# Attention: where the halves of side products and the parts of the shift stand among the slots

## The chip, the cores and the metric

The kernel runs on one core of a Trainium2 chip. A core has TensorE for matmuls (PE in the profile; its weight loads are PEld), VectorE (DVE), ScalarE (ACT), GpSimd (POOL) and SyncE (SP, which issues DMAs). Each works through its own instructions in their order and waits on semaphores for the others. The metric is device time in microseconds; lower is better.

## The reference

The whole program is a network of four layers on x of shape (4, 128, 64, 64): seven phases, one after the other. The change lies in the phase `attention`, the first half of the last layer: attention over the 4096 pixels of each of 4 images, with 4 heads of 32 channels, on a layer-normed x, and added to x.

```python
qkv = jnp.einsum('oc,bchw->bohw', w_qkv, x)
q, k, v = jnp.split(qkv, 3, axis=1)
...
q = to_heads(q) * SCALE
...
sim = jnp.einsum('bhdi,bhdj->bhij', q, k)
attn = jax.nn.softmax(sim, axis=-1)
out = jnp.einsum('bhij,bhdj->bhid', attn, v)
...
out = jnp.einsum('oc,bchw->bohw', w_out, out) + b_out[None, :, None, None]
```

and `x = x + _L3_conv_ref(_ln_c(x), ...)`. All of it is float32.

## The kernel before

**Tiles.** A batch (image) `b` has 4096 queries, in NCH = 8 chunks of CH = 512, and 4096 keys, in NT = 32 tiles of P = 128. A *block* `g` is one chunk of queries of one batch: 32 blocks in all, `b, c = divmod(g, NCH)`. A *slot* `t` is one tile of keys within a block: 32 slots in a block, 1024 in all.

**A slot.** The main loop (L2094 to L2132) records, in each slot and in this order: `scores(g, t)`, 4 matmuls (one a head, on four row groups of PE) into two *pairs*, PSUM tiles of two banks that hold two heads each (L1983 to L1988), and one exponential of ACT for each pair, into `att_ex` (L1990), with a bias `att_shift`; then `product` of the slot before (L2002), 4 matmuls of its exponentials with the values into `att_pv`; then `add_up` of the slot before, which adds its exponentials up: on DVE (L2021), or, for every fourth slot, by a DMA that accumulates, issued by POOL (L2019). `att_ex` has six buffers.

**PSUM.** There are 8 banks: three pairs (six banks), one bank `att_m`, one for `att_pv`. A call of `pair()` takes the next of the three. Each slot takes two.

**Side work.** What else must be computed on PE goes through the one bank `att_m` and is cut into *halves* of some 4 to 8 matmuls, each with its slot; after the second half, DVE or ACT reads the bank:

- `side`, the generator `project` (L1823): for the next batch, centred squares (ACT squares them) and their variances, an inverse root (one square root on ACT, four reciprocals on DVE, DMAs that spread it), then keys and queries of 8 chunks. It goes one step further in each slot of `USES` (L2088, L2116) in blocks 1 to 6 of a batch. Its steps in the second half also issue DMAs on SP.
- `values` (L1922): the values of 8 chunks, in slots of `USES` in block 0 and block 7.
- `total` (L2030): sums of the added-up exponentials over the keys, for the block before, after `join` has added DVE's part and the DMAs' part (L2024, a DMA issued by POOL); then `totalled` (a copy and two reductions), four `invert` (reciprocals, L2052), `scale_hidden` (a multiply on POOL, L2055), and `project_out` (L2064) with its addition to x. These stand in `queue` by slots after the block's last (L2136 to L2143).
- the shift of the next block: `begin` (L1946), twice, each with two small matmuls of scores into a pair and a maximum over them on DVE (L1962); then `gather_shift` (L1968) in slot 25 and `spread_shift` (L1976) in slot 27.

In block 0 a different rule, by `t % 4`, gives slots two halves each and every fourth slot none (L2110 to L2115).

**Order.** Inside `tc.manual_schedule` the instructions of PE, ACT, DVE and POOL stand in the order in which the program records them; the framework adds the semaphores.

Before the change, the slots with halves are 2 and 3, 6 and 7, 14 and 15, 18 and 19, 30 and 31 (`USES`), 10 and 11 (`total`), 22 and 23 (`project_out`); `begin` is in 19 and 23.

## Time and profile before

| | |
|---|---|
| median of 3 runs | 6059.14 us (6057.93 to 6070.12) |
| profiled execution, its own time | 6065.83 us |
| its span | 6063.9 us |
| mean granted clock of TensorE | 0.972 |
| stretch of the slots of attention | 3203 to 5656 us |
| in it, busy | PE 2445, DVE 2007, ACT 2163, POOL 304 us of 2453 |

The profile is of one execution. Times in a timeline are in us from the start of the span: start, length, engine, line, operation, tiles that it writes and reads, count; rows that follow each other on one engine are merged, and in brackets stands the idle time of the engine ahead of it with what ended it. In a group's row, "x8192 | 1291.7, 643 | 7.0 <-..." is the count, the busy time in us, the mean length in ns, and the idle time just before, with what ended it. Matmuls are pipelined, so that their lengths overlap; what a group takes is read from the start of the next one.

### The profile page before, as it was taken

What the parts mean: (1) busy time and instruction counts of PE and PEld (TensorE: products, weight loads), DVE (VectorE), ACT (ScalarE), POOL (GpSimd) and SP (SyncE); (2) the same over time, 40 slices, a digit from 0 to 9 for tenths busy, and PEclk for the clock granted to TensorE, in tenths of its full rate; (3) what the DMA queues carried; (4) which work ended last, traced back from release to release, by engine and by line L of the source; (5) the groups of instructions that cost most, each with busy time, mean ns of one, the idle gap of its engine ahead of it and who ended that gap; (6) DMA issues with size and microseconds to landing.
All of it is one profiled execution on the core that took longest, in us unless ns stands there. A gap on an engine that the chain in (4) does not pass through costs nothing. (4 is left out here: it accounts for less than half of the span.)

```text
span 6063.9 us, 97913 instructions
## 1 busy us (share of the span) xinstructions
PE 5701.8 (94%) x39923; PEld 2251.2 (37%) x39923; DVE 4383.8 (72%) x4739; ACT 3378.6 (56%) x4224; POOL 2056.5 (34%) x2015
## 2 busy tenths in 40 slices
PE   8999999879999988879979999999999999999799
PEld 2222222447667666433343222322232223222233
DVE  6888887456767666356446788888888888888666
ACT  4444444333323222421337888888888888999421
POOL 3989897027777777200000111111111111111000
PEclk9999999989999999989989999999999999999899
DMA  6434432068787877550274566656665666666200
GB/s 214 98 80 84 96 68 53 1 169 245 233 250 225 248 228 211 164 182 0 88 263 116 128 152 149 138 127 151 149 140 126 148 147 144 130 130 133 60 25 26
DMA packets 291038, 836.36 MB, mean 138 GB/s; under 512 B 43356, under 2 KB 117596, under 8 KB 244492
## 3 DMA queue, kind: packets, MB, share of 16 engines
q0 software_dynamic: 109568, 505.75, 35.0%
q1 hardware_dynamic: 181004, 324.17, 18.8%
q8 instruction: 320, 5.24, 0.4%
q14 instruction: 146, 1.20, 0.1%
HBM read 416.71 MB, written 111.10 MB: 87 GB/s over the span
## 5 line engine op out<-in xcount | busy, mean ns | idle before, releaser
L1990 ACT ACTIVATE att_ex<-att_sc,att_shift 128x1024 f32<-128x1024 f32 x2048 | 2141.6, 1111 | 288.9 <-PE att_sc L1986 173.5
L2021 DVE TENSOR_TENSOR att_dve<-att_dve,att_ex 128x2048 f32<-128x2048 f32 x704 | 1631.2, 2317 | 159.1 <-ACT att_ex L1990 134.1
L1986 PE MATMUL att_sc<-att_q,att_k 32*128 32x512 f32 x8192 | 1291.7, 643 | 7.0 <-ACT att_ex L1990 7.0
L2002 PE MATMUL att_pv<-att_ex,att_vals 128*32 128x512 f32 x8192 | 1095.9, 606 | 0.0
L969 POOL DMA_INDIRECT dcn_g<-dcn_table,dcn_idx x896 | 850.1, 949 | 363.9 <-issue 154.1
L412 DVE SCALAR_TENSOR_TENSOR inv_prod<-inv_pk,bspan,inv_seen 128x512 f32<-128x512 f32 (+1 forms) x1120 | 774.5, 743 | 140.2 <-PE inv_pk L399 139.9
L410 POOL TENSOR_TENSOR inv_prod<-inv_seen,inv_prod 128x512 f32<-128x512 f32 (+1 forms) x672 | 837.6, 1274 | 94.0 <-ACT inv_prod L409 94.0
L2019 POOL DMA_DIRECT2D att_dma<-att_ex x224 | 192.5, 860 | 1984.7 <-ACT att_ex L1990 1682.0
L409 ACT ACTIVATE inv_prod<-inv_pk,bspan 128x512 f32<-128x512 f32 (+1 forms) x672 | 436.1, 682 | 503.6 <-PE inv_pk L399 503.6
L977 DVE TENSOR_TENSOR dcn_g<-dcn_g,dcn_near_w 128x1024 f32<-128x1024 f32 x448 | 540.8, 1216 | 229.5 <-DMA dcn_g<-dcn_table,dcn_idx 212.9
L1986 PEld LDWEIGHTS att_sc<-att_q,att_k 32*128 32x128 f32 x8192 | 425.0, 184 | 673.7 <-issue 420.5
L986 PE MATMUL dcn_pt<-ident,dcn_g 128*128 128x128 f32 x3584 | 477.1, 277 | 62.6 <-DVE dcn_g L977 37.2
L399 PE MATMUL inv_pk<-inv_red,wtap 32*96 32x512 f32 (+1 forms) x3584 | 511.5, 636 | 7.2 <-DMA inv_seen<-inv_image 7.2
L986 PEld LDWEIGHTS dcn_pt<-ident,dcn_g 128*128 128x128 f32 x3584 | 418.6, 143 | 218.8 <-issue 132.7
L421 PE MATMUL inv_out<-inv_prod,inv_fold 96*32 96x512 f32 (+1 forms) x3584 | 478.1, 605 | 8.5 <-DVE xs L429 8.5
L2002 PEld LDWEIGHTS att_pv<-att_ex,att_vals 128*32 128x32 f32 x8192 | 161.8, 108 | 757.2 <-issue 732.0
L1092 ACT COPY dcn_st<-dcn_pt 128x512 f32<-128x512 f32 x224 | 129.7, 579 | 301.7 <-PE dcn_pt L986 301.7
L399 PEld LDWEIGHTS inv_pk<-inv_red,wtap 32*96 32x96 f32 (+1 forms) x3584 | 131.6, 170 | 385.3 <-DVE inv_prod L412 361.9
L1099 PE MATMUL dcn_out<-dcn_st,dcn_wk 128*128 128x512 f32 x448 | 235.4, 608 | 24.5 <-DVE xs L1107 24.5
L2491 PE MATMUL top_po<-top_xg,top_we 128*128 128x512 f32 x512 | 233.2, 599 | 0.0
L1005 ACT ACTIVATE dcn_fold<-dcn_pf,dcn_turn 128x256 f32<-128x256 f32 x128 | 60.2, 473 | 298.8 <-PE dcn_pf L1001 298.8
L421 PEld LDWEIGHTS inv_out<-inv_prod,inv_fold 96*32 96x32 f32 (+1 forms) x3584 | 71.0, 108 | 356.3 <-issue 333.9
(433 smaller groups left out, 5441.4 us busy)
## 6 DMA issues: line engine op xcount, KB each, us to landing
att_dma<-att_ex POOLq DMA_DIRECT2D x224, 1024.0 KB, 7.0
inv_seen<-inv_image SPq DMA_DIRECT2D x256, 266.0 KB
moe_w<-in_L_ffn_weight SPq DMA_DIRECT2D x64, 1024.0 KB
dcn_table<-dcn_xt SPq DMA_DIRECT2D x64, 512.0 KB
att_dma<-att_ex SPq DMA_DIRECT2D x32, 1024.0 KB
att_dve<-att_dma POOLq DMA_DIRECT2D x32, 1024.0 KB, 9.5
moe_table<-moe_xt SPq DMA_DIRECT2D x64, 288.0 KB
dcn_g<-dcn_table,dcn_idx POOLq DMA_INDIRECT x896, 3.8
```

The costliest lines, as they stand in the source:

```text
L399: nc.tensor.matmul(pk[0:m], wtap[half][rg, i, blk], red[rg, h * CH : (h + 1) * CH], start=True, stop=True)
L409: nc.scalar.activation(prod[0:m, h], pk[0:m], AF.Identity, bias=by)
L410: nc.gpsimd.tensor_mul(of, view, of)
L412: nc.vector.scalar_tensor_tensor(out=of, in0=as_shape(pk[0:m], of), scalar=by, in1=view, op0=ALU.add, op1=ALU.mult)
L421: nc.tensor.matmul(po[CR * blk : CR * (blk + 1), h, :], fold[0:m], prod[0:m, h, :], start=unit == 0, stop=unit == UNITS - 1,)
L969: nc.gpsimd.indirect_dma_start(out=g[:, t, :], out_offset=None, in_=rows, in_offset=bass.IndirectOffsetOnAxis(ap=idx[:, Q4 * c + i + t, k ...
L977: nc.vector.tensor_mul(near, near, by)
L986: nc.tensor.matmul(pt[0][:, (i + t) * P : (i + t + 1) * P], near[:, t, q, :], net.ident, is_transpose=True, start=i + t + q == 0, stop=i + ...
L1986: nc.tensor.matmul(pes[h // 2][:, h % 2, :], ks[r, t * P : (t + 1) * P], q[r], start=True, stop=True)
L1990: nc.scalar.activation(ex[:, 2 * two : 2 * two + 2, :], pes[two], AF.Exp, bias=shifts[g][:, two : two + 1],)
L2002: nc.tensor.matmul(block["pv"][r], vals[:, t, r], ex[:, h, :], start=t == 0, stop=t == NT - 1)
L2021: nc.vector.tensor_add(block[who], block[who], ex)
```

## The change

The three pairs become three named tiles that are handed round in turn by `pair()`. `begin` uses the tile whose turn is next, without moving the turn, so that the scores that follow start in the same tile. `begin` moves from slots 19 and 23 to 18 and 22. `USES` becomes 1 and 3, 5 and 7, 13 and 15, 17 and 19, 29 and 31; the halves of `total` go to slots 9 and 11, those of `project_out` to 21 and 23. So each half stands in an odd slot, and the second halves in the same slots as before.

```diff
+            pairs = [ps.tile([P, 2, CH], F32, name=f"att_sc{i}", bufs=1) for i in range(3)]
+
             def pair():
-                return ps.tile([P, 2, CH], F32, name="att_sc", tag="sc", bufs=3)
+                pairs.append(pairs.pop(0))
+                return pairs[-1]
...
                 q = state[b][0][c]
-                pm = pair()
+                pm = pairs[0]
...
-                USES = [t for two in (2, 6, 14, 18, 30) for t in (two, two + 1)]
+                USES = [t for four in (0, 4, 12, 16, 28) for t in (four + 1, four + 3)]
...
-                        if g + 1 < NG and t in (19, 23):
+                        if g + 1 < NG and t in (18, 22):
                             begin(g + 1, t // 4 - 4)
...
                         if c == 0 and g > 0 and t in USES[0:8]:
-                            values(b, 4 + USES.index(t) // 2, t % 2)
+                            values(b, 4 + USES.index(t) // 2, t % 4 // 2)
                         if c == NCH - 1 and b + 1 < B and t in USES[2:10]:
-                            values(b + 1, USES.index(t) // 2 - 1, t % 2)
+                            values(b + 1, USES.index(t) // 2 - 1, t % 4 // 2)
...
                     for half in range(2):
-                        at(slot + 11 + half, total, block, half)
-                        at(slot + 23 + half, project_out, block, g, half)
+                        at(slot + 10 + 2 * half, total, block, half)
+                        at(slot + 22 + 2 * half, project_out, block, g, half)
```

`slot` is there the number of the block's last slot, so `slot + 10` is slot 9 of the next block.

## The prediction

> **What bounds the kernel now.** I read the page first, for the engines and the costliest groups; then the busy time in stretches, for where attention lies (3203 to 5656 us: 1024 slots, 2.40 us each); then the timeline of PE slot by slot, for what a slot costs; then the timelines of DVE and POOL around the steps that move.

> ```profile
> PE 5701.8 (94%) x39923; PEld 2251.2 (37%) x39923; DVE 4383.8 (72%) x4739; ACT 3378.6 (56%) x4224; POOL 2056.5 (34%) x2015
> ...
> L1990 ACT ACTIVATE att_ex<-att_sc,att_shift 128x1024 f32<-128x1024 f32 x2048 | 2141.6, 1111 | 288.9 <-PE att_sc L1986 173.5
> ...
> L1986 PE MATMUL att_sc<-att_q,att_k 32*128 32x512 f32 x8192 | 1291.7, 643 | 7.0 <-ACT att_ex L1990 7.0
> ```

> PE is nearly always busy and ACT has slack (288.9 us idle, mostly until scores are there). But a busy PE is not a PE at its peak: a wait can hide inside a group of overlapping matmuls, so the starts of the groups count. Slots 8 to 11 of block 10:

> ```profile
> 4004.01 1.14 PE L1986 MATMUL att_sc<-att_q,att_k 32*128 32x512 f32 x8
> 4005.08 1.07 PE L2002 MATMUL att_pv<-att_ex,att_vals 128*32 128x512 f32 x8
> 4006.07 1.46 PE L1986 MATMUL att_sc<-att_q,att_k 32*128 32x512 f32 x8
> 4007.46 1.07 PE L2002 MATMUL att_pv<-att_ex,att_vals 128*32 128x512 f32 x8
> 4008.46 1.14 PE L1986 MATMUL att_sc<-att_q,att_k 32*128 32x512 f32 x8
> 4009.53 1.07 PE L2002 MATMUL att_pv<-att_ex,att_vals 128*32 128x512 f32 x8
> 4010.41 0.61 PE L2035 MATMUL att_m<-att_dve,att_ones_f 128*32 128x256 f32 x8
> 4010.96 1.14 PE L1986 MATMUL att_sc<-att_q,att_k 32*128 32x512 f32 x8
> ```

> From scores to scores: slot 8 (plain) 2.07, slot 9 (plain) 2.38, slot 10 (with a half) 2.50. So a half costs 0.43 us of PE, and a plain slot's successor pays 0.31 more: its scores last 1.46 in place of 1.14. The reason: ACT starts some 1.22 us after the scores (4013.46 to 4014.68 two slots on), one activation takes 1.11, and only its end frees the buffer for the second pair of the next scores: 1.22 + 1.11 and about 0.05 of signalling are 2.38, but after a plain slot PE is there after 2.07. After 2.50 (a half) nothing waits; after 2.38 nothing either. Of two plain slots the second pays. After slots 2, 6, 10 ... (two beyond a multiple of four) ACT starts sooner and the wait is 0.26: slot 3 of block 27, which has no halves there, lasts 2.33.

> **Does work in the successor swallow the wait?** This decides the change. Slot 25 shows it:

> ```profile
> 4044.74 1.45 PE L1986 MATMUL att_sc<-att_q,att_k 32*128 32x512 f32 x8
> ...
> 4047.12 0.38 PE L1968 MATMUL att_m<-ident,att_low 128*1 128x128 f32 x2
> 4047.43 1.14 PE L1986 MATMUL att_sc<-att_q,att_k 32*128 32x512 f32 x8
> ...
> 4049.50 1.40 PE L1986 MATMUL att_sc<-att_q,att_k 32*128 32x512 f32 x8
> ```

> Slot 24 is plain (its scores start at 4042.67, 2.07 earlier); slot 25 pays the wait (1.45) and then the gather on top: 2.69 = 2.38 + 0.31. Slot 26, plain again, again 2.07; slot 27's scores wait again (1.40). This is "side work in every second slot" already, and every second scores group waits. In block 0, slot 3 is plain and slot 4, with two halves, lasts 3.19 where its neighbours with two halves last 2.93: 0.26 is paid there too.

> **The change, slot by slot.** Now the halves of blocks 1 to 31 stand in pairs: one wait after each plain pair, nine in a full block (slots 1, 5, 9, 13, 17, 21, 25, 27, 29; 28 pays 0.19 behind the spread). After the change all halves stand in odd slots, and each odd slot follows a plain one, so each pays, except 19 and 23: there `begin` lengthens the slot ahead. A `begin` costs 0.44 now (slot 19: 2.94 against 2.50), so slots 18 and 22 become 2.51 and 2.52, long enough. In a full block:

> - pairs (0,1), (4,5), (8,9), (12,13), (16,17), (20,21): 2.07 + 2.38 + 0.43 = 4.88 each, 29.25 with unrounded rows
> - pairs (2,3), (6,7), (10,11), (14,15), (30,31): 2.07 + 2.33 + 0.43 = 4.83 each, 24.13
> - (18,19): 2.51 + 2.50 = 5.01; (22,23): 2.52 + 2.50 = 5.02
> - (24,25): 2.07 + 2.69 = 4.76; (26,27): 2.07 + 2.34 = 4.41; (28,29): 2.26 + 2.40 + 0.43 = 5.09

> Sum 77.65, against 76.36 now (scores of slot 0 of block 9 at 3908.76, of block 10 at 3985.12): +1.29. Counted so, 12 blocks (1, 2, 4, 5 of batches 0 to 2) are full: +15.5. Block 3 of a batch, with its square root and reciprocals in place of three halves: 3 x 0.7. Block 6, whose halves end after slot 15: 75.86 against 75.51, 3 x 0.35 (plain pairs are 2.07 + 2.38 or 2.33; with slot 19 plain behind `begin`, the wait passes to slot 20, 2.31, and 21 is 2.50). Blocks with eight `values` halves (block 7 of three batches, block 0 of three): 76.8 against 75.8 to 76.1, 6 x 0.95. Blocks 25 to 30, with only totals and output projections: 73.28 against 73.71, 6 x -0.43, since `begin` now ends a wait that nothing else ended. Block 0 and the last: +0.5 each. **Sum of the PE terms: +22.8 us.**

> **What the moved steps wait for.** The reduction in `begin` (L1962, 0.41 us) moves up one slot, and with the kept turn the first pair of the next scores waits for it; everything of PE is queued behind. DVE comes to it late: from the totals on (slot 11) it works without a pause. In block 27:

> ```profile
> 5328.89 0.94 DVE L2052 RECIPROCAL att_inv<-att_inv 128x128 f32<-128x128 f32 x1
> ```

> The chain from the copy of the totals (5313.97) to the end of that reciprocal (5329.76, where the next instruction starts) is 15.8 us; then the moved reduction follows. After the change, slot 18's scores come 13.3 us after slot 12's in such a block, so the reduction ends 3.1 us into slot 18, while the next scores are due after 2.51: 0.6 late in blocks 25 to 30, by the same count 0.5 in block 6, 0.1 where an eviction after slot 15 lengthens the chain but slots 13, 15 and 17 are longer too (15 blocks), nothing in blocks 1 and 2 of a batch. Sum 9 x 0.55 + 15 x 0.1 = **+6.5**. Bounds: 0 if the chain starts earlier, and one more reciprocal's 0.87 in each of 24 blocks, 21, if it slips behind.

> The output projection's first half moves from slot 22 to 21 and needs `att_hidden` from POOL. In block 4:

> ```profile
> 3578.18 3.10 POOL L2055 TENSOR_TENSOR att_hidden<-att_hidden,att_inv 128x512 f32<-128x512 f32 x1 [2.75 <-DVE att_inv L2052]
> ```

> POOL ends at 3581.28, which is 4.97 after slot 20's scores (3576.31); the half is issued at 3582.71. One slot earlier it is due 2.07 + 2.27 = 4.34 after slot 20: 0.7 late with signalling. This holds in the 15 blocks where an eviction follows slot 19; elsewhere POOL ends earlier. **+10.5**. Bounds: 0, if POOL takes the 1.26 us that it takes in blocks 1, 2, 9, 10, 17, 18, and 1.15 each, 17, if a whole addition (2.29) is ahead of those 1.26.

> [...]

> At nothing I cost: the totals' first half in slot 9, since the join's DMA lands by slot 8 (9 to 12 us after its issue in slot 3); the DMAs of the projection steps, which stay with their second half in slots 3, 7, 15, 19, 31 and so keep their place in SP's queue (only the spreading in block 3 of a batch moves, from slot 6 to 5, ten slots ahead of its first reader on DVE); the named buffers themselves, since the same ACT wait stands ahead of the second pair. Without the cover of the join a total would cost up to its landing time, 9 us a block.

> The granted clock was 1.00 over block 9 with nine short waits in it. [...]

> **Sum:** 22.8 + 6.5 + 10.5 = +39.8 us. The profiled execution took 6065.8 (span 6063.9), 6.7 above the median of the runs shown. On that median: 6059.1 + 39.8 = **6099 us**, 0.66% slower. Own range: 6076 (PE terms less a quarter, no late DVE or POOL) to 6126 (PE terms, both upper bounds, and 6 for the spread of runs).

> **Rivals.**

> *The half covers the wait (faster).* One place: the second pair of an odd slot's scores. ACT's slack speaks for it: with a longer slot in every two it could be ahead. Then no odd slot waits and a full block takes 32 x 2.07 + 14 x 0.43 + 0.31 + 0.25 + 0.89 = 73.6; with 2.7 less in 24 blocks and 4.4 in six, 5967 us. Against it: slots 25 to 27 above; the wait is counted from the same slot's scores, not from a backlog. It decides once the wait falls by more than 0.11 (about 350 waits against 40 us). 7%.

> *`begin` gives back more (no change).* The profile names some 32 us in which the weight load of `begin` stood waiting for ACT (62 times). Were that PE's own time, the move would return it and the sum would be about +7: 6067. Against it: slot 19's 0.44 is all work, as its scores and matmuls follow each other without a hole. 5%.

> *DVE becomes the bound (much slower).* If the reduction of slot 18 falls behind one more addition (2.29 us) in 24 blocks, scores, products and activations stand for it: +55, less what is counted, 6147. For it: DVE has no pause from slot 12 to 21. Against: its place in DVE's order, ahead of that addition. 9%.

> *My forecast* gets 79%. With 0.2% (12 us), about what can be told from no change here: faster 0.07, same 0.06, slower 0.87. The range 6076 to 6126 leaves out the two outer rivals.

> **What would show it.** Right: odd slots' scores at 1.40 to 1.46, pairs of slots of 4.83 and 4.88, slots 18 and 22 at 2.51 and scores of 19 and 23 at 1.14; a full block of 77.7 (blocks 1 and 2 of a batch) or 78.4 (4 and 5); PE waiting for `att_low` after slot 18 and for `att_hidden` in slot 21. Wrong: odd scores at 1.14, or pairs of 4.57.

## The result, and the profile after

| | before | after |
|---|---|---|
| median | 6064.10 us (6057.93 to 6070.12, 4 runs) | 6100.51 us (6096.77 to 6107.2, 4 runs) |
| profiled execution: span | 6063.9 us | 6102.0 us |
| from the span's start to the first slot | 3203.1 us | 3207.8 us |
| first to last slot of attention | 2449.6 us | 2483.6 us |

The changed kernel takes 1.0064 times as long, interval [1.0052, 1.0077]: 36 us slower. Of the 38.1 us between the two spans 34.0 lie in the slots. 4.7 lie ahead of them, in code that the change doesn't touch, where executions differ by more than that: the first slot began between 3198.4 and 3212.2 us in the four further profiles with the same code there (`spare`, `halves`, `unlate`, `again1`). Behind the slots it is 0.6 less.

The page after, engines and costliest groups:

```profile
PE 5723.1 (94%) x39923; PEld 2274.4 (37%) x39923; DVE 4382.7 (72%) x4739; ACT 3379.6 (55%) x4224; POOL 2041.0 (33%) x2015
...
L1993 ACT ACTIVATE att_ex<-att_sc,att_shift 128x1024 f32<-128x1024 f32 x2048 | 2140.6, 1112 | 322.8 <-PE att_sc L1989 204.8
...
L1989 PE MATMUL att_sc<-att_q,att_k 32*128 32x512 f32 x8192 | 1312.8, 641 | 10.7 <-ACT att_ex L1993 6.7
```

The same instructions, the same count; ACT takes 1.0 us less than before and stands idle 33.9 us longer. The scores on PE last 21.1 us longer in sum at nearly the same mean (641 against 643 ns), so it is their overlap that has changed. PE's timeline of slots 8 to 11 of block 10 shows where:

```profile
4021.28 1.14 PE L1989 MATMUL att_sc<-att_q,att_k 32*128 32x512 f32 x8
4022.35 1.07 PE L2005 MATMUL att_pv<-att_ex,att_vals 128*32 128x512 f32 x8
4023.34 1.45 PE L1989 MATMUL att_sc<-att_q,att_k 32*128 32x512 f32 x8
4024.72 1.07 PE L2005 MATMUL att_pv<-att_ex,att_vals 128*32 128x512 f32 x8
4025.61 0.61 PE L2038 MATMUL att_m<-att_dve,att_ones_f 128*32 128x256 f32 x8
4026.15 1.14 PE L1989 MATMUL att_sc<-att_q,att_k 32*128 32x512 f32 x8
4027.22 1.06 PE L2005 MATMUL att_pv<-att_ex,att_vals 128*32 128x512 f32 x8
4028.22 1.41 PE L1989 MATMUL att_sc<-att_q,att_k 32*128 32x512 f32 x8
```

Slot 8 is plain, 2.07 us from scores to scores. Slot 9 has the half of the sums, and yet its scores last 1.45, and it is 2.81 long. Slot 10 is plain again, and slot 11's scores wait again (1.41). Every odd slot with a half pays the wait and the half, except 19 and 23, which follow a piece of the shift. The rows from 4045.57 on are slots 18 and 19 of that block: 2.51 and 2.50, with scores of 1.14 in both:

```profile
4045.57 1.14 PE L1989 MATMUL att_sc<-att_q,att_k 32*128 32x512 f32 x8
4046.53 0.62 PE L1960 MATMUL att_sc<-att_q,att_k 32*128 32x128 f32 x4
4047.08 1.06 PE L2005 MATMUL att_pv<-att_ex,att_vals 128*32 128x512 f32 x8
4048.08 1.14 PE L1989 MATMUL att_sc<-att_q,att_k 32*128 32x512 f32 x8
```

The two steps that came late show too. PE in slot 21 of block 4, and POOL at the same time:

```profile
3587.23 1.06 PE L2005 MATMUL att_pv<-att_ex,att_vals 128*32 128x512 f32 x8
3588.79 0.64 PE L2067 MATMUL att_m<-att_hidden,att_wo 128*32 128x256 f32 x8 [0.50 <-POOL att_hidden L2058]
```

```profile
3585.64 3.09 POOL L2058 TENSOR_TENSOR att_hidden<-att_hidden,att_inv 128x512 f32<-128x512 f32 x1 [2.46 <-DVE att_inv L2055]
```

The half of the output projection is issued 2.95 us after its slot's scores (3585.84) and not 2.27: the slot lasts 3.52 in 15 blocks, and 2.81 in blocks 1 and 2 of a batch, where POOL's multiply takes 1.27 us (1.60 in block 17) and is over sooner. In block 27, scores of slot 19 wait for the reduction of the shift's piece, which stands behind a reciprocal on DVE; slot 18 lasts 3.05, 0.54 more than in block 10:

```profile
5367.99 1.14 PE L1989 MATMUL att_sc<-att_q,att_k 32*128 32x512 f32 x8 [0.38 <-DVE att_low L1965]
```

### The profile page after: what moved, and what is told of

Its sections match the earlier page's. It is cut to its first block, busy times and chain, and to the rows that moved or that the text cites. A ratio compares the mean times of both kernels' runs of the same rounds, so it can differ in the third digit from the quotient of the medians.

```text
span 6102.0 us, 97906 instructions
## 1 busy us (share of the span) xinstructions
PE 5723.1 (94%) x39923; PEld 2274.4 (37%) x39923; DVE 4382.7 (72%) x4739; ACT 3379.6 (55%) x4224; POOL 2041.0 (33%) x2015
## 5 line engine op out<-in xcount | busy, mean ns | idle before, releaser
L1989 PE MATMUL att_sc<-att_q,att_k 32*128 32x512 f32 x8192 | 1312.8, 641 | 10.7 <-ACT att_ex L1993 6.7
L1989 PEld LDWEIGHTS att_sc<-att_q,att_k 32*128 32x128 f32 x8192 | 450.5, 183 | 675.9 <-issue 601.3
```

What stands on the lines that cost most here:

```text
L1989: nc.tensor.matmul(pes[h // 2][:, h % 2, :], ks[r, t * P : (t + 1) * P], q[r], start=True, stop=True)
```

## The experiments

In slot lengths, "block" means a full one (the second or third chunk of a batch) unless another is named. `turn` and `keep` ran on another chip, on which the kernel before took 6258.23 us, and in the profiles of the two the first slot begins only at some 3400 us; their plain slots are as long as elsewhere (2.07), so they are read by their slots and by their ratio to before.

### Does work in a slot swallow the wait? (`spare`)

The kernel before, with halves that nothing reads:

```diff
+            def spare():
+                pd = bank()
+                for q in range(4):
+                    r = slice(32 * q, 32 * q + 32)
+                    nc.tensor.matmul(pd[r, 0 : CH // 2], wo[:, r], wqkv[:, 0 : CH // 2], start=True, stop=True)
...
+                        if g > 0 and t in (5, 8, 12, 13, 24):
+                            spare()
```

> The kernel before, with five further halves of four matmuls in blocks 1 to 31, whose result nobody reads: in slots 5, 8, 24 alone and in 12 and 13 together. Theory (the wait follows a plain slot that itself did not wait, and work in the waiting slot is paid on top): slots 4, 5, 6 of block 2 at 2.07, 2.81, 2.50; slots 8, 9, 10 at 2.50, 2.07, 2.81 (the wait moves from 9 to 10); slots 12 and 13 at 2.50 and 2.50 (the wait is gone, two halves cost 0.55 in place of 0.86); slots 24 and 25 at 2.50 and 2.38 (0.12 more than before). Together +1.5 us a block, some +47 us. Rival (a half is swallowed by the wait of its own slot): slot 5 at 2.50, slot 25 still at 2.69, and together +1.2 or less a block.

Measured: 6106.19 us, one run, beside 6061.5 before. A full block lasts 77.84, 1.47 more than before (1.5 expected). Slots 4, 5, 6 lasted 2.07, 2.81, 2.50; 12 and 13 2.50 each; 24 and 25 2.50 and 2.38; slots 8, 9, 10 2.50, 2.07, 2.76. PE's timeline for these last three:

```profile
4018.64 1.14 PE L1986 MATMUL att_sc<-att_q,att_k 32*128 32x512 f32 x8
4019.71 1.06 PE L2002 MATMUL att_pv<-att_ex,att_vals 128*32 128x512 f32 x8
4020.59 0.61 PE L2058 MATMUL att_m<-att_wqkv,att_wo 128*32 128x256 f32 x8
4021.14 1.14 PE L1986 MATMUL att_sc<-att_q,att_k 32*128 32x512 f32 x8
4022.21 1.07 PE L2002 MATMUL att_pv<-att_ex,att_vals 128*32 128x512 f32 x8
4023.21 1.41 PE L1986 MATMUL att_sc<-att_q,att_k 32*128 32x512 f32 x8
```

With a half added (L2058) slot 8 is 2.50 and slot 9 no longer waits (1.14, before 1.46); plain slot 9 now hands the wait on to slot 10, which has a half and pays all the same (1.41). The half stands behind its slot's scores in PE's order, so it ends the wait of the next slot's scores, in none of these places its own.

### The change in three parts (`halves`, `turn`, `keep`)

`halves` takes from the change the places of the halves alone:

```diff
-                USES = [t for two in (2, 6, 14, 18, 30) for t in (two, two + 1)]
+                USES = [t for four in (0, 4, 12, 16, 28) for t in (four + 1, four + 3)]
...
-                        at(slot + 11 + half, total, block, half)
-                        at(slot + 23 + half, project_out, block, g, half)
+                        at(slot + 10 + 2 * half, total, block, half)
+                        at(slot + 22 + 2 * half, project_out, block, g, half)
```

> The changed kernel with the halves in odd slots, but begin as before: in slots 19 and 23, in a buffer taken from the ring. Theory: slots 18 and 22 are plain again and so 19 and 23 pay 0.26 to 0.31 each, while the reduction is no longer late in slot 18; +15 for the first, -6 for the second, so about 9 us slower than the changed kernel, some 44 us above before (ratio 1.007). Rival (the loss comes from begin's earlier place and the buffer that keeps its turn): within 10 us of before (ratio 1.000 to 1.002).

Measured: 6116.99 us (6116.01 to 6122.1), ratio 1.0099 [1.0083, 1.0114]; slots 2504.8 us in sum, 55.2 above before and 21.2 above the changed kernel, where 9 had been expected. Of these 21.2 us 7.9 lie in blocks 3, 11 and 19, whose length varies for a reason of its own (below); 13.3 are left. Slots 19 and 23 lasted 3.34, not 3.2: in a slot that waits, a piece of the shift costs 0.58 (before: 2.91 against 2.33 in block 25, slot 19), not 0.44.

`turn` is the changed kernel whose shift piece takes a turn of the three pairs again:

```diff
-                pm = pairs[0]
+                pm = pair()
```

> The changed kernel with one part undone: the shift's piece takes a turn of the three score buffers again, as before, but stays in slots 18 and 22. Then the next slot's second pair of scores waits for the end of the second activation of the slot ahead, 1.22 + 2 x 1.11 + 0.05 = 3.49 us after that slot's scores. Theory (the kept turn is what lets the piece lengthen a slot without a half at no other cost): with slot 18 at 2.51 the second pair of slot 19 is 0.43 late (0.24 is what slot 20 pays in blocks 25 to 30 before), so slots 19 and 23 last 2.75 to 2.95 instead of 2.50: 0.5 to 0.9 us a block, +15 to +26 us, about 6115 to 6126 us. Rival (the place alone did it, the turn is worth nothing): slots 19 and 23 at 2.50, no change against the changed kernel.

Measured: ratio 1.0130 [1.0113, 1.0146], slots 2530.3 us. Slots 19 and 23 lasted 3.33 and 3.37. The rival falls, but the cost is twice what I expected: 1.61 us a block more than in the changed kernel, 46.7 us in sum, 38.9 without blocks 3, 11 and 19, which vary by themselves. PE's timeline of slots 18 and 19 of block 10:

```profile
4244.26 1.14 PE L1989 MATMUL att_sc<-att_q,att_k 32*128 32x512 f32 x8
4245.22 0.62 PE L1960 MATMUL att_sc<-att_q,att_k 32*128 32x128 f32 x4
4245.77 1.06 PE L2005 MATMUL att_pv<-att_ex,att_vals 128*32 128x512 f32 x8
4246.77 1.97 PE L1989 MATMUL att_sc<-att_q,att_k 32*128 32x512 f32 x8
```

The scores of slot 19 last 1.97. Their single records, which this view merges, begin at 4246.77 and 4247.30 for the first pair of heads and at 4247.61 and 4248.14 for the second, which waits for the activation that ends at 4247.56. In slot 18, where nothing waits, all four heads begin together (4244.26 to 4244.28, and again from 4244.79). So the second pair is due with the first, not 0.55 later as I had reckoned, and a wait takes the heads apart: 0.84 late here, 0.31 in every plain slot's successor.

`keep` is the kernel before with the kept turn alone (with the list of three named tiles, as in the changed kernel):

```diff
-                return ps.tile([P, 2, CH], F32, name="att_sc", tag="sc", bufs=3)
+                pairs.append(pairs.pop(0))
+                return pairs[-1]
...
-                pm = pair()
+                pm = pairs[0]
```

> The kernel before with one part added: the shift's piece borrows the score buffer that is next and keeps its turn, still in slots 19 and 23; all halves stay where they were. Theory: there the turn saves next to nothing, since slot 19 with a half and a piece lasts 2.94 and the next second pair comes 0.55 later, at 3.49, when the second activation has just ended; only blocks 25 to 30, where slot 20 pays 0.24, can gain, and where VectorE is late with the piece's reduction the slot behind can lose: the slots' sum stays within 6 us of 2449.6, the time within 0.2% of before. Rival (the turn is worth a gain by itself): over 12 us faster than before.

Measured: ratio 1.0001 [0.9991, 1.0010], slots 2445.9 us. Where slot 19 has a half and a piece it gains nothing. The 3.7 us less than before lie in blocks 3, 11 and 19 (-4.7 together), which are taken up below.

Without blocks 3, 11 and 19, the slots' sum goes up by 50.1 us for the halves' places, by 25.7 more when the pieces move to 18 and 22 with the old turn, and down by 38.9 with the kept turn: +36.9 for the whole change. The kept turn is worth much, but only once a piece stands in a slot without a half; the loss is that of the halves' places.

### Taking the late steps away (`unlate`)

The changed kernel, with the output projection's halves back in 22 and 23, and the two reductions over the sums (DVE) after the reciprocals:

```diff
-                nc.vector.tensor_reduce(most[:, g : g + 1], block["inv"], AX.X, ALU.max)
-                nc.vector.tensor_reduce(least[:, g : g + 1], block["inv"], AX.X, ALU.min)
+
+            def extremes(block, g):
+                nc.vector.tensor_reduce(most[:, g : g + 1], block["inv"], AX.X, ALU.max)
+                nc.vector.tensor_reduce(least[:, g : g + 1], block["inv"], AX.X, ALU.min)
...
-                        at(slot + 22 + 2 * half, project_out, block, g, half)
+                        at(slot + 23 + half, project_out, block, g, half)
...
+                    at(slot + 29, extremes, block, g)
```

> The changed kernel with the two late steps taken out of the way: both halves of the output projection in slots 22 and 23 as before, and the two reductions over the sums in slot 28, over their reciprocals (the bound tested is the same), so that DVE's chain ahead of slot 18 is 1.2 us shorter. Theory: slot 21 at 2.38 in place of 3.52 in the 15 blocks where it waited for POOL, slot 22 0.43 longer, slot 18 at 2.51 in place of 3.05 in blocks 6, 14, 22 and 25 to 30; 10.5 and 5 us, so 15 us faster than the changed kernel, some 21 us above before (ratio 1.0035). Rival (those waits are covered by ACT's slack and come back in the next slot): no faster than the changed kernel (1.006).

Measured: 6095.71 us (6092.93 to 6109.5), ratio 1.0061 [1.0048, 1.0075]; a miss. Slot 21 fell to 2.38 as expected, and blocks 4 and 5 of a batch gained 0.57. In blocks 25 to 30 slot 18 fell from 3.05 to 2.60; in block 6 of a batch it stayed at 2.98. Without blocks 3, 11 and 19 the slots' sum is 4.4 us below the changed kernel's, where 15 had been expected. The larger part of what is missing lies in slot 22: with a half and a piece it took 3.02 to 3.35 us where 2.95 was counted on. All engines over slots 21 and 22 of block 10, in part:

```profile
4054.22 4.20 ACT L1993 ACTIVATE att_ex<-att_sc,att_shift 128x1024 f32<-128x1024 f32 x4
...
4058.46 0.30 PEld L1960 LDWEIGHTS att_sc<-att_q,att_k 32*128 32x128 f32 x4 [0.71 <-ACT att_ex L1993]
...
4059.28 0.42 DVE L1965 TENSOR_REDUCE att_low<-att_sc 128x1 f32<-128x256 f32 x1
...
4060.52 0.71 PE L1989 MATMUL att_sc<-att_q,att_k 32*128 32x512 f32 x4
```

The tile that the piece borrows is the one that slot 21's second activation still reads, and that ends at 4058.42, since slot 21 is now shorter. The piece starts behind it, at 4058.46, and all that follows on PE moves with it. In the slots of 3.02, 3.09 and 3.35 us the piece starts 0.97, 1.03 and 1.29 us into the slot, each time 0.05 to 0.06 after that activation, and the slot ends 2.05 to 2.06 later. DVE is not what holds it here: its reduction is over at 4059.70, and the next scores start at 4060.52. In block 4 the reduction ends 0.73 us later in its slot, which is 3.09 long all the same. So the wait for POOL, taken out of slot 21, came back in part as a wait for ACT in slot 22.

### Side work in every slot (`quarters`, `quarters2`)

If a plain slot hands on a wait, no slot should be plain. `quarters` cuts each half in two, in slots 0 to 11 and 16 to 23, and the sums into slots 12 to 15; the pieces, with the kept turn, go to 24 and 25, the projection to 28 to 31:

```diff
-                for h in range(2):
-                    part = slice(h * CH // 2, (h + 1) * CH // 2)
+                for h in range(4):
+                    part = slice(h * P, (h + 1) * P)
...
-                USES = [t for four in (0, 4, 12, 16, 28) for t in (four + 1, four + 3)]
+                USES = [t for four in (0, 4, 8, 16, 20) for t in range(four, four + 4)]
...
-                        if g + 1 < NG and t in (18, 22):
-                            begin(g + 1, t // 4 - 4)
+                        if g + 1 < NG and t in (24, 25):
+                            begin(g + 1, t - 24)
```

> All halves cut into quarters, one in each slot: side steps in slots 0 to 11 and 16 to 23, totals in 12 to 15, begin in 24 and 25, the gather in 26, the spread in 27, the output projection in 28 to 31; named buffers as in the changed kernel. Theory: a quarter costs 0.22, so nearly each slot lasts 2.28 and only 0.05 to 0.10 of the wait of 2.33 or 2.38 is left in every second: a full block about 74.7 in place of 76.4 before, blocks 25 to 30 about 1 us less; some 45 us faster than before (ratio 0.9925). Rival (a group of matmuls has a fixed cost, as begin with two small ones costs 0.44 and the gather 0.31): a quarter 0.32, +2.8 us a full block, no faster than before (1.000 to 1.005).

Measured: 6047.19 us (6041.15 to 6053.86), ratio 0.9978 [0.9969, 0.9987]: faster than before, by less than expected. Slots with a quarter lasted 2.28 and 2.33 to 2.38, as counted (some 2.5 in slots 5, 9, 13 and 21 of blocks 1 and 2 of a batch); a full block 75.8 to 76.3, where 74.7 was expected. Slots 24 and 25 took 2.65 and 3.03 instead of 2.51 each; PE and DVE there in block 10:

```profile
4040.99 1.06 PE L2005 MATMUL att_pv<-att_ex,att_vals 128*32 128x512 f32 x8
4042.49 0.71 PE L1989 MATMUL att_sc<-att_q,att_k 32*128 32x512 f32 x3 [0.44 <-DVE att_low L1965]
```

```profile
4037.56 0.94 DVE L2055 RECIPROCAL att_inv<-att_inv 128x128 f32<-128x128 f32 x1
4038.65 0.42 DVE L1965 TENSOR_REDUCE att_low<-att_sc 128x1 f32<-128x256 f32 x1
4038.99 3.11 DVE L2024 TENSOR_TENSOR att_dve<-att_dve,att_ex 128x2048 f32<-128x2048 f32 x1
4042.03 0.41 DVE L1965 TENSOR_REDUCE att_low<-att_sc 128x1 f32<-128x256 f32 x1
```

The second reduction waits for an addition of 3.11 us. `quarters2` has the sums four slots earlier, so that the reciprocals are over by slot 19, and the reductions over the sums in slot 28:

```diff
-                USES = [t for four in (0, 4, 8, 16, 20) for t in range(four, four + 4)]
+                USES = [t for four in (0, 4, 12, 16, 20) for t in range(four, four + 4)]
...
-                        at(slot + 13 + half, total, block, half)
+                        at(slot + 9 + half, total, block, half)
...
-                        at(slot + 18 + 2 * i, invert, block, i)
+                        at(slot + 14 + 2 * i, invert, block, i)
...
+                    at(slot + 29, extremes, block, g)
```

> The quarters again, with the side steps moved so that VectorE has done its reciprocals before the shift's pieces begin: sums in slots 8 to 11, reciprocals in 13, 15, 17 and 19, side products in quarters in slots 0 to 7 and 12 to 23, the shift's score pieces in 24 and 25, its two sum reductions in slot 28, output projection in quarters in 28 to 31. Theory (what the first quarters kernel lost in slots 24 and 25, 2.65 and 3.03 us, was VectorE's reciprocals ahead of the pieces' reductions): slots 24 and 25 come to 2.5 to 2.7 us each, about 0.5 us a full block less than in the first quarters kernel, some 16 us in all; ratio to before about 0.995. Rival (the pieces' reductions are late for another reason, or quarters themselves cost more than they save): the slots stay above 2.9 us in sum of excess and the ratio stays at 0.998 or goes above 1.

Measured: 6026.78 us (6020.81 to 6033.4), ratio 0.9940 [0.9926, 0.9953]; slots 2413.5 us, 19.2 below `quarters`. Slots 24 and 25 lasted 2.64 and 2.52. DVE there in block 10:

```profile
4032.13 0.42 DVE L1965 TENSOR_REDUCE att_low<-att_sc 128x1 f32<-128x256 f32 x1 [1.01 <-PE att_sc L1960]
4032.47 2.28 DVE L2024 TENSOR_TENSOR att_dve<-att_dve,att_ex 128x2048 f32<-128x2048 f32 x1
4034.67 0.42 DVE L1965 TENSOR_REDUCE att_low<-att_sc 128x1 f32<-128x256 f32 x1
```

The first reduction now finds DVE idle (1.01 us), and the second starts 0.13 us after its piece's matmuls, which end at 4034.54; the scores of the next slot are no longer held up. By its ratio this kernel is faster than the one of before and than `quarters`.

### The block with the square root (`again1`)

One term of the prediction had the wrong sign: blocks 3, 11 and 19 together took 2.9 us less than before, where I had counted 4.5 more. There ACT loads tables twice (1.28 us each) around a square root (0.72 us), and the scores stand for 2.2 to 2.3 us. PE in block 3, before and after:

```profile
3455.45 1.13 PE L1986 MATMUL att_sc<-att_q,att_k 32*128 32x512 f32 x4
3458.86 2.04 PE L1986 MATMUL att_sc<-att_q,att_k 32*128 32x512 f32 x4 [2.28 <-ACT att_ex L1990]
3460.84 1.93 PE L2002 MATMUL att_pv<-att_ex,att_vals 128*32 128x512 f32 x8
```

```profile
3461.05 1.13 PE L1989 MATMUL att_sc<-att_q,att_k 32*128 32x512 f32 x4
3464.42 1.13 PE L1989 MATMUL att_sc<-att_q,att_k 32*128 32x512 f32 x4 [2.24 <-ACT att_ex L1993]
3465.47 1.07 PE L2005 MATMUL att_pv<-att_ex,att_vals 128*32 128x512 f32 x8
```

The pause is the same to 0.04 us; before, the matmuls behind it take about twice as long. The question was whether the steps' places do that. `again1` is the changed kernel once more, unedited.

> The changed kernel itself once more, for the two blocks with the square root (blocks 3, 11, 19, whose first slots took 31.1, 31.1 and 32.4 us in the changed kernel's profile and 33.7 to 34.0 in the one of before). Theory: the third slot of these blocks varies between executions of one and the same program, from 5.4 to about 7.3 us, and is above about 5.5 us just where the granted TensorE clock fell to 0.50 behind the pause of 2.2 to 2.3 us; so at least one of the three lies on the other side than in the first profile. Rival (the places of the steps decide it): 5.42 us in blocks 3 and 11 again, with the clock at 1.00, and a drop in block 19 alone.

Measured: 6106.43 us, one run. Slot 3 of the three blocks lasted 5.73, 5.42 and 5.51 (5.42, 5.42, 5.43 in the first profile), slot 4 3.34, 2.07 and 3.56 (2.07, 2.07, 3.64). Block 3 has crossed over, and 7.3 was not reached here (`unlate` had 7.24 in block 19, `halves` 7.23 in block 11). A row of the windows has the stretch, its length, the busy times of PE, PEld, DVE, ACT and POOL with their counts, then the granted clock, the DMA share and GB/s. Slots 3 and 4 of block 3 in the first profile and in `again1`:

```profile
3461.03:3468.56 7.53, 5.29 (x38) 1.25 (x34) 6.59 (x6) 7.18 (x8) 0.85 (x1) 1.00 0.77 174
```

```profile
3460.29:3469.40 9.11, 6.87 (x39) 1.49 (x36) 7.74 (x6) 7.49 (x9) 0.85 (x1) 0.81 0.83 222
```

And in `halves`, whose steps stand in the same places in this part of the block:

```profile
3451.66:3462.30 10.64, 8.40 (x39) 1.54 (x35) 7.73 (x6) 8.03 (x9) 0.85 (x1) 0.69 0.73 199
```

The same instructions take 7.53, 9.11 or 10.64 us, with a granted clock of 1.00, 0.81 or 0.69. The changed program took both of the first two values in block 3, and in its first execution block 19 lost the clock (0.81 over 9.11 us) where blocks 3 and 11, with the same steps, kept it. So the places of the steps don't decide it.

The clock's own records show what does. In all ten traces the granted clock changes only on a grid of 3.413 us that runs through the whole trace: before, the three stretches of half clock (0.50) in the slots start at 3458.94, 4073.34 and 4687.73 us, 180 steps apart, and each lasts two steps; in the changed kernel's first profile there is one in the slots, of one step. Rows for two steps around the pause of block 3 and for two around that of block 19, in that profile (the first number after the comma is PE's busy time, the 1.00 or 0.50 the clock):

```profile
3460.15:3463.56 3.41, 2.03 (x12) 0.36 (x12) 1.59 (x2) 3.37 (x4) 0.85 (x1) 1.00 0.21 43
3463.56:3466.97 3.41, 2.55 (x16) 0.77 (x20) 3.41 (x4) 3.41 (x4) 0.00 (x0) 1.00 1.14 231
4712.85:4716.26 3.41, 1.98 (x12) 0.46 (x12) 3.41 (x3) 3.40 (x5) 0.30 (x1) 1.00 0.82 166
4716.26:4719.67 3.41, 3.41 (x20) 0.72 (x16) 3.30 (x3) 2.14 (x3) 0.00 (x0) 0.50 0.99 262
```

The same pause of 2.24 us is cut differently by the grid. After a step with 1.38 us of idle PE the clock stays; after one with 1.43 us the next step runs at half clock. This holds throughout: of the some 7150 steps at full clock in the slots of the ten traces, 23 had 1.42 to 2.29 us of idle, and each was followed by half clock; the others had at most 1.39 us, and none was. So in these traces the phase of the grid decided. By an estimate from these numbers, a pause of 2.24 or 2.28 us escapes when a grid line falls into its middle 0.5 to 0.6 us, about one time in six, whichever kernel it is (7 of the 30 pauses did).

## Why the prediction was right

Its terms, in us, beside the slots of the two profiles (after less before):

| blocks | predicted | measured |
|---|---|---|
| 1, 2 of a batch: 6 x 1.29 | 7.7 | 8.2 |
| 4, 5 of a batch: 6 x (1.29 + 0.1 + 0.7) | 12.5 | 12.3 |
| 3 of a batch: 3 x (0.7 + 0.8) | 4.5 | -2.9 |
| 6 of a batch: 3 x (0.35 + 0.5) | 2.6 | 3.2 |
| with `values`: 6 x (0.95 + 0.8) | 10.5 | 11.7 |
| 25 to 30: 6 x (-0.43 + 0.55) | 0.7 | 0.1 |
| first and last | 1.0 | 1.4 |

- **The waits of the odd slots**: right. Pairs of slots took 4.88 and 4.83, as forecast; a full block 77.74 (forecast 77.65). `spare` shows the rule by itself and `halves` that it is where the loss comes from. What the prediction said of its cause, the second pair's buffer, stands; `turn` adds that the two pairs are due together. Without blocks 3, 11 and 19 the rows above come to 35.0 predicted and 36.9 measured.
- **The late reduction**: right where it was put. Slot 18 lasted 3.05 in block 25 (0.54 late, forecast 0.6) and 2.54 or 2.55 in 14 of the 15 blocks (0.04, forecast 0.1; block 24 took 2.89). That the row of blocks 25 to 30 comes so near is partly luck: in the profile before, ACT waited 0.69 to 1.22 us for an accumulating DMA in blocks 26, 28 and 29, which made them longer by chance. A block without such a wait went from 73.71 to 73.96, 0.25 more, where 0.12 was forecast.
- **The late `att_hidden`**: right, 0.71 in 15 blocks against 0.7. The row is 3.09 us; with the projection a slot later (`unlate`) slot 21 falls to 2.38. In the profile before, the multiply took 3.10 or 3.11 us in the 25 blocks where an addition on DVE had begun 0.26 us before it, and 1.26 to 1.42 in the six where one began 0.20 to 0.28 us after it.
- **Block 3 of a batch**: 4.5 against -2.9. I took the slot lengths of the profile before for the place's own; they held three drops of the clock of two steps each, and the profile after held one of one step. This is 7.4 us; the other rows together came out 1.9 higher, and the slots' sum is 34.0, where the rows come to 39.5 (the forecast's 39.8 but for rounding). Without a drop on either side the term is about right: block 11 of `keep`, where the halves stand as before and the kept turn adds 0.02 to a full block, took 78.85, and block 3 of the changed kernel 80.49, 1.64 more, where 1.5 was forecast.
- **At nothing**: the sums' half in slot 9 did not wait for the join in a full block; slot 9 is 2.81, as slot 1 is. Elsewhere slot 9 was at times longer (4.17 in block 7 of `again1`). The added waits cost no clock in the profile after: it was 1.00 over every block but 0 (0.964, a drop that began ahead of the slots, at 3193.9 us) and 19 (0.979, behind the square root).
- **The rivals.** "The half covers the wait" falls by the scores of 1.45 and 1.41. "`begin` gives back more": from `halves` to the changed kernel the pieces' move and the kept turn regain 21.2 us (13.3 without blocks 3, 11 and 19), but slots 18 and 19 came to the 5.01 that the forecast had counted, not to less. "DVE becomes the bound" did not come in this kernel, and did, in part, in `quarters`.

## What to carry to other kernels

When two engines hand buffers round in turn and the added work stands behind the instruction that waits, as it does here, it is not hidden in the slot that waits (slot 9 of the changed kernel is 2.81, 2.38 and 0.43): it delays the waiting engine's next request, so what it saves is the wait of the slot after it (in `spare` slot 9's scores last 1.14 and not 1.46). A wait taken away in one slot can come back in the next, as in `unlate` (slot 21 at 2.38 in place of 3.52, slot 22 at 3.02 to 3.35 where 2.95 was counted on). Read the start-to-start times of a plain slot, of its successor and of a filled slot (2.07, 2.38 and 2.50 here) from the timeline before anything is moved; side work was cheapest here when it was cut so finely that hardly a slot arrived early, and when the small reductions that it needed found their engine free (`quarters2`, ratio 0.9940). And before a difference between two profiles is put down to the change, compare the granted clock of the stretches in question (here 1.00, 0.81 and 0.69 went with 7.53, 9.11 and 10.64 us for the same instructions).
